# Turning the row maxima on VectorE and laying them under the queries through memory, with the blank rows written behind the first expert's up weights

## The chip, the cores and the metric

The kernel runs on one core of a Trainium2 chip. A core has TensorE (matmuls), VectorE, ScalarE and GpSimd, a sync engine that only issues transfers, and 16 DMA engines that move data between the chip's memory and the core's on-chip memory. Times are device microseconds from start to end of one execution; the median of three runs before the change is 941.17 us (939.94 to 942.25). In what follows PE is TensorE, PEld its weight load, DVE is VectorE, ACT is ScalarE, POOL is GpSimd and SP the sync engine; ACTq and SPq are the instructions with which ACT and SP issue transfers.

## The reference

Eight sequences of 256 tokens, 512 channels, all in float32. One layer: attention of the tokens on a context, then a feed-forward part with a shared expert and eight routed ones, two for each token.

```python
x = x + xattn(layernorm(x), ctx, ctx, Wq, Wk, Wv, Wfc, bfc)   # 32 heads of 16, 8 groups of keys
x = x + ffn(layernorm(x), ...)

# xattn
score = einsum('bhqd,bhkd->bhqk', qh, kh) / sqrt(16)
attn = softmax(score, axis=-1)                                 # subtracts the maximum of each row
out = einsum('bhqk,bhkd->bhqd', attn, vh) ... @ Wfc.T + bfc
# ffn
scores = softmax(h @ gate_weight.T)                            # 8 experts in 4 groups
topk_w, topk_i = group_limited_topk(scores)                    # 2 groups, then 2 experts
routed = sum over the two experts of topk_w * (silu(h @ gate_w.T) * (h @ up_w.T)) @ down_w.T
shared = silu(h @ sh_gate_w.T) * (h @ sh_up_w.T) @ sh_down_w.T
return routed + shared
```

## The kernel before, in words

**Attention.** The work of attention is cut into units: a sequence has eight, made of two groups of key heads, two pairs of query heads and two halves of 128 queries or keys. Each unit k is done twice. In a "max" step (`maxima`, L948) PE computes the scores of 128 queries against 256 keys for eight heads, 16 small matmuls into a PSUM tile `s` of four banks, and DVE takes the negated maximum of each row (L964, the tile `nm`). In an "exp" step (`weights`, L980) PE computes the same scores the other way round, keys on the partitions. The query tile `qT` has a 17th row under the 16 channels of each head, which holds the negated maxima, and the key tile has ones there, so the matmul of 17 rows gives scores from which the maximum has been taken off. ACT takes their exponential (L996). `values` (L1001) multiplies them with the values.

Between the two steps stands `place` (L966): the maxima have the queries on the partitions, but the 17th row needs them along the row. PE turns two blocks of 128 x 8 by a matmul with the identity into a PSUM tile `tn` of the pool `ps_m` (L972), ACT copies 8 x 256 numbers to `nmT` (L976), and ACT issues one transfer into the 17th rows (L978). There are 32 such places, one for every two units.

**The order.** PE, ACT, DVE and SP run in the order in which the program is written; only GpSimd's order is left to the scheduler. The list `order` alternates max and exp steps, the max step four units ahead (LAG = 4), and starts the first two sequences with four max steps in a row. After the matmuls of a step, `beside` (L1330) puts in what is due: for two finished exponentials the products with the values (in max steps after the start), then the places. A place is put in one step after the second maxima of its pair. What else there is to do (projections of later sequences, the output product `close`, the router, the shared expert's `pieces`) stands in a list of stages, and `fill` takes pieces of it, each with a cost in microseconds, until the step is at least `gap - work` and at most `most - work` long. `work` counts what `beside` put in: in an exp step 0.44 for a place. If nothing is ready in the first 44 steps, `warm` puts in two idle matmuls. `others.passed(cost)` tells the stages that time has gone by. The pool `ps_m` has three PSUM buffers, shared by all these pieces and by `tn`.

**The routed experts.** The router sends each token's normed row with `send` (L1173) to two places of a table `rows` in memory, one region for each expert. `plan` works out on DVE where each expert's rows end (`t_end`, L1185) and which blocks of 128 rows there are to do. SP then issues, in this order: the first expert's up weights (L381) and down weights (L384), the first block of rows (`load`, L407 and L413: four transfers of 128 x 128 numbers in 32 x 32 blocks, and a fifth with routing weights and token numbers), blocks and weights of experts 1 and 2, and then, for each expert, 64 blank rows written behind the last one in use (L575, at a row number that SP reads from `t_end`). The loads read the same table as the blank rows are written to, and the row numbers are known on the chip only, so a load waits for blank rows issued before it and blank rows wait for loads issued before them. After that come the shared expert's kept values for the last sequence (L199) and, in `run`, the weights of experts 3, 4 and so on, each set one tile ahead of its block of rows.

`run` goes through the tiles. In each, DVE turns the next block of rows (`turn`, L434), PE computes gate and up (`up`, L468), DVE multiplies them (L485), PE does the down product of the tile before (`down`, L499), and `turn_act` turns the product (L491 on PE, L493 and L494 on DVE). As DVE works in order, the product of tile n (L485) stands behind the turn of block n + 1. At the very end the shared expert's down product for the last sequence is added to what is in memory and written out by SP (L647, L654, L655).

Of the kernel before, what the change touches and what calls it, by code (L numbers as in the profile page):

```python
# [43 lines left out]
F32 = mybir.dt.float32  # L44
I32 = mybir.dt.int32
ENG = mybir.EngineType
# [4 lines left out]
P = 128  # L51
# [33 lines left out]
@with_exitstack  # L85
def xattn_ffn(
    ctx: ExitStack,
    tc: tile.TileContext,
    x: bass.AP,
    ctxT: bass.AP,  # L90
    wq: bass.AP,
    wkv: bass.AP,
    wfc: bass.AP,
    bfc: bass.AP,
    wgate: bass.AP,
    wsg: bass.AP,
    wsd: bass.AP,
    wgu: bass.AP,
    wd: bass.AP,
    out: bass.AP,  # L100
):
    nc = tc.nc

    ctx.enter_context(tc.manual_schedule(engines={ENG.PE, ENG.Activation, ENG.DVE, ENG.SP}))

    keep = ctx.enter_context(tc.tile_pool(name="keep", bufs=1))
    dram = ctx.enter_context(tc.tile_pool(name="dram", bufs=1, space=bass.MemoryType.DRAM))
    ps_m = ctx.enter_context(tc.tile_pool(name="ps_m", bufs=3, space=PSUM))
    right = ctx.enter_context(ExitStack())
    left = ctx.enter_context(ExitStack())  # L110

    ident = keep.tile([P, P], F32, name="ident")
    make_identity(nc, ident)


    t_exp = keep.tile([P, N_PLAN], I32, name="t_exp")
    t_row = keep.tile([P, N_PLAN], I32, name="t_row")
    t_one = keep.tile([P, N_PLAN, N_EXP], F32, name="t_one")
    t_all = keep.tile([P, 1], I32, name="t_all")

    t_end = keep.tile([P, N_EXP], I32, name="t_end")

    blank = dram.tile([R, W], F32, name="blank")
    rows = dram.tile([N_EXP * S_R + P, W], F32, name="rows")


    kept = dram.tile([P, len(SCH), S], F32, name="kept")

    feed = Shared(right, tc, ps_m, wsg, wsd, out, kept)
    tail = attention(  # L130
        left, tc, ps_m, feed, x, ctxT, wq, wkv, wfc, bfc, wgate, out, ident,
        rows, t_exp, t_row, t_one, t_all, t_end, blank,
    )
    left.close()
    routed(
        ctx, tc, ps_m, wgu, wd, wsd, kept, ident,
        rows, t_exp, t_row, t_one, t_all, t_end, blank, out, tail, right,
    )
# [215 lines left out]
def routed(  # L354
# [25 lines left out]
    def up_weights(e):  # L380
        nc.sync.dma_start(wgu_all[:, e], wgu[e])  # L381
# [91 lines left out]
                    stop=(c == NC - 1),  # L473
                )

    def up(i):
        of_expert(i)
        gu = [ps_g.tile([P, F], F32, tag=f"g{k}", name=f"rg{i}_{k}") for k in range(2)]
        for k in range(2):
            product(gu[k], i, slice(k * F, (k + 1) * F))  # L480
        del xTs[i]
        sg = place(work, [P, F], "sg", f"rsg{i}")
        nc.scalar.activation(sg, gu[0], AF.Silu)  # L483
        acts[i] = place(work, [P, F], "act", f"ract{i}")
        nc.vector.tensor_mul(acts[i], gu[1], sg)  # L485
# [76 lines left out]
        add_up(o, i)  # L562

    up_weights(0)
    down_weights(0)

    load(0)
    for e in (1, 2):
        load(e)
        up_weights(e)  # L570
        down_weights(e)

    for e in range(N_EXP):
        to = value(t_end, e, ENG.SP, N_EXP * S_R)
        alone(tc, nc.sync.dma_start(rows[bass.ds(to, R), :], blank).ins)  # L575
    while tail.cost < tail.total - 2 * 0.88:
        tail.step()
    turn(0)
# [30 lines left out]
    def run(tiles):  # L609

        halfs = [n for n, i in enumerate(tiles) if i >= N_EXP + N_FULL]
        when = [N_EXP - 3, *(n + 3 for n in halfs)]
        for n, i in enumerate(tiles):
            if 3 <= n + 2 < len(tiles):
                load(tiles[n + 2])
            if i + 3 < N_EXP:
                up_weights(i + 3)
                down_weights(i + 3)
            for k, at in zip(halfs, when):
                if at == n:  # L620
                    second(tiles[k])
            if n + 1 == len(tiles):
                last(i, tiles[n - 1])
                break
            if n == halfs[-1] + 2:
                down_sh, act_sh = two(len(SCH), D, len(SCH), S)
                nc.sync.dma_start(down_sh, wsd)
                nc.sync.dma_start(act_sh, kept)
            if n > 0:
                turn(tiles[n + 1])  # L630
            up(i)
            if n > 0:
                down(tiles[n - 1])
            else:
                turn(tiles[n + 1])
            turn_act(i)

        sums = []
        for q in range(QC):
            t0 = ((B - 1) * QC + q) * P  # L640
            to = out[t0 : t0 + P, :]
            sums.append((to, work.tile([P, D], F32, tag=f"sum{q}", bufs=1, name=f"sum{q}")))
            nc.sync.dma_start(sums[q][1], to)
        for q, (to, y) in enumerate(sums):
            ps = ps_m.tile([P, D], F32, tag="m", name=f"o{B - 1}_{q}")
            for i in range(len(SCH)):
                nc.tensor.matmul(  # L647
                    ps,
                    lhsT=act_sh[:, i, q * P : (q + 1) * P],
                    rhs=down_sh[:, i],  # L650
                    start=(i == 0),
                    stop=(i == len(SCH) - 1),
                )
            nc.vector.tensor_add(y, ps, y)  # L654
            nc.sync.dma_start(to, y)  # L655
        more()

    full = [N_EXP + k for k in range(N_FULL)]
# [5 lines left out]


def attention(
    ph, tc, ps_m, feed, x, ctxT, wq, wkv, wfc, bfc, wgate, out, ident,
    rows, t_exp, t_row, t_one, t_all, t_end, blank,
):

# [271 lines left out]
    def unit(k):  # L942
# [2 lines left out]
        G, k = divmod(k, UNITS // NG)  # L945
        return b, G, k // QC * 2, k % QC

    def maxima(k):  # L948
        b, G, j0, qc = unit(k)
        qT, kT = qTs[b], kTs[b % DEEP]  # L950
        ps = ps_s.tile([P, 4, 2, S], F32, tag="s", name=f"s1_{b}_{G}_{qc}_{j0}")
        for j in range(2):
            for r in range(4):
                band = slice(32 * r, 32 * r + HD)
                nc.tensor.matmul(  # L955
                    ps[:, r, j],
                    lhsT=qT[band, G, j0 + j, qc * P : (qc + 1) * P],
                    rhs=kT[band, G],
                    start=True,
                    stop=True,  # L960
                )
        if qc == 0:
            nms[b, G, j0] = small.tile([P, QC, 4, 2], F32, tag="nm", bufs=3, name=f"nm{b}_{G}_{j0}")
        nc.vector.tensor_reduce(nms[b, G, j0][:, qc], ps, AX.X, ALU.max, negate=True)  # L964

    def place(k):  # L966

        b, G, j0, _ = unit(k)
        nm = nms.pop((b, G, j0))
        ps = ps_m.tile([P, S], F32, tag="m", name=f"tn{b}_{G}_{j0}")  # L970
        for qc in range(QC):
            nc.tensor.transpose(  # L972
                ps[: 2 * 4, qc * P : (qc + 1) * P], nm[:, qc].rearrange("p r j -> p (r j)"), ident
            )
        row = small.tile([2 * 4, S], F32, tag="nmT", bufs=1, name=f"nmT{b}_{G}_{j0}")
        nc.scalar.copy(row, ps[: 2 * 4])  # L976
        under = qTs[b].rearrange("(r x) g j s -> r x g j s", x=32)[:, HD, G, j0 : j0 + 2]
        nc.scalar.dma_start(under, row)  # L978

    def weights(k):  # L980
        b, G, j0, kc = unit(k)
# [348 lines left out]
    def beside():  # L1330

        for k in to_sum if len(to_sum) == QC else ():
            values(k, ex.pop(k))
            others.passed(1.0)
            b, k = divmod(k, UNITS)
            if k == UNITS - 1:
                closed(b)
            if k % QC == QC - 1:
                to_sum.clear()
        for k in to_place:  # L1340
            place(k)
            others.passed(0.22)
        to_place.clear()

    def closed(b):
# [40 lines left out]
    for i, (what, k) in enumerate(order):  # L1386
        dull = warm if i < 44 else None
        if what == "max":
            if k % UNITS == 0:
                others.finish(projected[k // UNITS])  # L1390

            copy.free = "ACT"
            maxima(k)
            others.passed(1.0)

            gap = 3.2 if len(to_sum) == QC else 2.6
            work = 1.0 * (len(to_sum) == QC) * QC
            beside()
            if k % QC == QC - 1:
                to_place.append(k)  # L1400
            most = 4.6
        else:

            copy.free = "DVE"
            now = k
            ex[k] = weights(k)
            others.passed(1.1)
            gap = 2.1
            work = 1.0 * (len(to_sum) == QC) * QC + 0.44 * len(to_place)
            beside()  # L1410
            to_sum.append(k)
            most = 4.3 if k + LAG < n else 6.0
        others.fill(now, gap - work, most - work, dull)
        if i >= 2:
            next(loads, None)
# [75 lines left out]
```

## Time and profile before

| what | value |
|---|---|
| median of three runs | 941.17 us |
| the profiled execution, in all | 938.76 us |
| its span, first to last instruction | 937.0 us |
| PE busy | 910.8 us (97%) |
| DVE busy | 475.0 us (51%) |
| ACT busy | 182.3 us (19%) |
| POOL busy | 134.3 us (14%) |
| granted TensorE clock over the span | 0.993 |
| attention's units, first max to last exp | about 23 to 567 us |
| routed experts, first to last matmul | 635 to 920 us |

Busy time of PE includes overlap: matmuls are pipelined and their ends are modelled. The page of the profile divides the span in 40 slices of 23.4 us and gives the busy share of each engine in tenths, the clock that TensorE was granted and the busy share of the DMA engines. A view by lines lists groups of equal instructions; a timeline lists single instructions with start and duration, and in square brackets how long the engine had been idle and what released it.

### The profile page before, as it was taken

To read this page: it belongs to the slowest core of one execution; us is meant where nothing else is said; L and a number is where in the kernel's file an instruction comes from. 1 tells how busy PE (TensorE), PEld (TensorE's weight loads), DVE (VectorE), ACT (ScalarE), POOL (GpSimd) and SP (SyncE) were. 2 spreads that over 40 slices of the span, in tenths; PEclk is the share of its full clock that TensorE was granted. 3 is DMA by queue.
4 is the path that set the end of the run, shared out by engine and by line. 5 is a ranking of instruction groups with operands and counts; after the bars stand their busy time and mean duration, and the time that the engine had idled before them with its cause. 6 is when DMAs were issued, how large, how long until landed. Compare 5 with 4: busy or idle time off the path is not lost.

```text
span 937.0 us, 13140 instructions
## 1 busy us (share of the span) xinstructions
PE 910.8 (97%) x4865; PEld 531.1 (57%) x4865; DVE 475.0 (51%) x1063; ACT 182.3 (19%) x222; POOL 134.3 (14%) x171
## 2 busy tenths in 40 slices
PE   9999999999999999999999999999599999999997
PEld 8775565536445554654654544775355555555553
DVE  4554867566755856654675655382233333333331
ACT  1224123223223222222222241101000000000000
POOL 4000100201101101010120121030012212121211
PEclk9999999999999999999999999999799999999999
DMA  6366620201102021011111011069995364644623
GB/s 223 86 180 220 192 46 2 82 6 35 48 13 81 24 46 47 1 53 35 36 48 35 13 48 57 12 219 294 347 341 105 69 164 71 157 78 87 149 38 75
DMA packets 59266, 90.45 MB, mean 97 GB/s; under 512 B 13312, under 2 KB 39680, under 8 KB 57152
## 3 DMA queue, kind: packets, MB, share of 16 engines
q1 hardware_dynamic: 50512, 70.63, 24.7%
q0 software_dynamic: 7648, 17.83, 9.4%
q10 hardware_dynamic: 1040, 1.12, 0.4%
q8 instruction: 41, 0.67, 0.3%
q14 instruction: 25, 0.20, 0.1%
HBM read 57.88 MB, written 27.24 MB: 91 GB/s over the span
## 4 chain that ended last, share of the span: by engine, by line
PE 89%; DVE 4%; DMA 3%; SPq 1%; issue 1%; ACT 1%; POOL 0%; ACTq 0%; DVEq 0%; POOLq 0%
PE rg L468 16%; PE gu L181 14%; PE ro L499 9%; PE o L205 8%; PE s L988 7%; PE s L955 7%; PE fc L1046 6%; PE pq L921 6%; PE av L1007 6%; PE pkv L865 2%; DVE nm L964 1%; PE pkv L854 1%; PE ra L491 1%; PE o L647 1%; PE tn L972 1%; PE warm L1279 1%
## 5 line engine op out<-in xcount | busy, mean ns | idle before, releaser
L964 DVE TENSOR_REDUCE nm<-s 128x8 f32<-128x2048 f32 x64 | 146.6, 2290 | 86.2 <-PE s L955 82.0
L468 PE MATMUL rg<-wgu_all,rxT 128*128 (+2 forms) x552 | 171.3, 464 | 1.1 <-DVE rxT L434 0.9
L181 PE MATMUL gu<-hT,gu_w 128*128 128x256 f32 x704 | 166.6, 385 | 0.0
L996 ACT ACTIVATE ex<-s 128x2048 f32<-128x2048 f32 x64 | 120.1, 1877 | 225.7 <-PE s L988 216.0
L181 PEld LDWEIGHTS gu<-hT,gu_w 128*128 128x128 f32 x704 | 129.1, 190 | 40.9 <-issue 24.6
L468 PEld LDWEIGHTS rg<-wgu_all,rxT 128*128 128x128 f32 (+1 forms) x552 | 100.6, 187 | 56.4 <-issue 8.8
L499 PE MATMUL ro<-wd_all,raT 128*128 (+5 forms) x210 | 96.5, 594 | 0.0
L513 POOL DMA_INDIRECT y<-ry,rid x38 | 58.4, 1537 | 239.5 <-DVE ry L510 156.0
L205 PE MATMUL o<-down,act 128*128 128x512 f32 x168 | 79.6, 604 | 0.3 <-DVE q L346 0.3
L988 PE MATMUL s<-qT,kT 17*128 17x512 f32 x512 | 73.0, 640 | 2.0 <-DVE nm L964 1.9
L955 PE MATMUL s<-kT,qT 16*128 16x256 f32 x1024 | 73.4, 400 | 1.5 <-ACT ex L996 0.8
L483 ACT ACTIVATE rsg<-rg 128x352 f32<-128x352 f32 x34 | 15.8, 464 | 253.2 <-PE rg L468 246.0
L955 PEld LDWEIGHTS s<-kT,qT 16*128 16x128 f32 x1024 | 46.3, 184 | 30.9 <-ACT ex L996 14.1
L499 PEld LDWEIGHTS ro<-wd_all,raT 128*128 128x128 f32 (+3 forms) x210 | 38.4, 186 | 42.9 <-issue 35.5
L921 PE MATMUL pq<-xT,wq_sb 128*128 128x256 f32 x256 | 61.2, 386 | 0.5 <-DVE acc L214 0.3
L1007 PE MATMUL av<-ex,v 128*32 128x512 f32 x512 | 61.5, 598 | 0.0
L1046 PE MATMUL fc<-wfc_sb,o 128*128 128x512 f32 x128 | 60.9, 604 | 0.1
L1173 POOL DMA_INDIRECT rows<-lnf,idx x32 | 31.7, 991 | 201.0 <-DVE idx L1167 190.2
L485 DVE TENSOR_TENSOR ract<-rg,rsg 128x352 f32<-128x352 f32 x34 | 17.8, 523 | 84.0 <-PE rg L468 84.0
L510 DVE TENSOR_SCALAR ry<-ro,rw 128x512 f32<-128x512 f32 x35 | 26.3, 750 | 66.7 <-PE ro L499 66.7
L921 PEld LDWEIGHTS pq<-xT,wq_sb 128*128 128x128 f32 x256 | 46.6, 190 | 14.5 <-issue 6.0
L205 PEld LDWEIGHTS o<-down,act 128*128 128x128 f32 x168 | 29.4, 190 | 35.8 <-issue 34.5
(184 smaller groups left out, 710.0 us busy)
## 6 DMA issues: line engine op xcount, KB each, us to landing
wgu_all<-wgu SPq DMA_DIRECT2D x8, 1408.0 KB
xs<-rows SPq DMA_DIRECT2D x128, 64.0 KB
wd_all<-wd SPq DMA_DIRECT2D x8, 768.0 KB
two<-wgu SPq DMA_DIRECT2D x3, 1408.0 KB
cT<-ctxT SPq DMA_DIRECT2D x8, 512.0 KB
acc<-x SPq DMA_DIRECT2D x16, 256.0 KB
y<-acc SPq DMA_DIRECT2D x16, 256.0 KB
x<-x SPq DMA_DIRECT2D x14, 256.0 KB
```

Of the source, the lines that this page charges most:

```text
L181: nc.tensor.matmul(ps[:, i], lhsT=self.gu[k][:, c, i * P : (i + 1) * P], rhs=hT[:, c], start=(c == 0), stop=(c == NC - 1),)
L205: nc.tensor.matmul(ps, lhsT=act[:, k, q * P : (q + 1) * P], rhs=self.down[:, k], start=(i == 0), stop=(i == len(SCH) - 1),)
L468: nc.tensor.matmul(dst[part], lhsT=xTs[i][:, c, part.start // BAND : part.stop // BAND], rhs=w, start=(c == 0), stop=(c == NC - 1),)
L499: nc.tensor.matmul(o[part], lhsT=aTs[i][:fn, fc, part], rhs=w, start=(fc == 0), stop=(fc == len(FCH) - 1),)
L513: nc.gpsimd.indirect_dma_start(out=out, out_offset=bass.IndirectOffsetOnAxis(ap=to, axis=0), in_=y[part], in_offset=None, compute_op=ALU.add,)
L921: nc.tensor.matmul(ps[:, i], lhsT=wq_sb[:, c, part], rhs=xT[:, c], start=(c == 0), stop=(c == NC - 1),)
L955: nc.tensor.matmul(ps[:, r, j], lhsT=qT[band, G, j0 + j, qc * P : (qc + 1) * P], rhs=kT[band, G], start=True, stop=True,)
L964: nc.vector.tensor_reduce(nms[b, G, j0][:, qc], ps, AX.X, ALU.max, negate=True)
L988: nc.tensor.matmul(ps[:, r], lhsT=kT[band, G, kc * P : (kc + 1) * P], rhs=qT[band, G, j0 : j0 + 2], start=True, stop=True,)
L996: nc.scalar.activation(ex, ps, AF.Exp, scale=HD**-0.5)
L1007: nc.tensor.matmul(av[32 * r : 32 * r + 32], lhsT=vs[b % DEEP][:, kc, 4 * G + r], rhs=ex[:, r], start=(kc == 0), stop=(kc == QC - 1),)
L1046: nc.tensor.matmul(ps, lhsT=o[:, c, qc * P : (qc + 1) * P], rhs=wfc_sb[:, c], start=(c == 0), stop=(c == NC - 1),)
```

## The change

It has four parts.

1. `place` no longer uses PE, PSUM and an ACT copy. The maxima of a pair of units are written to one of three fixed tiles of 128 x 32, set to zero once by GpSimd, in 16 of its 32 columns. DVE turns the tile in blocks of 32 x 32, and ACT issues a transfer of the whole turned tile (128 pieces of 32 numbers) to a buffer in memory. One step later a new function `take` lets ACT issue a second transfer, from that buffer into the 17th rows. The filler's account of a place (0.44 in `work`, 0.22 in `passed`) is gone.
2. The eight writes of blank rows stand between the first expert's up weights and its down weights.
3. The first tile's turn of the product (`turn_act` of tile 0) stands between the gate and the up product of tile 1.
4. The last writes of the output are issued by ACT.

```diff
-    def up(i):
+    def up(i, between=None):
         of_expert(i)
...
         for k in range(2):
             product(gu[k], i, slice(k * F, (k + 1) * F))
+            if k == 0 and between is not None:
+                turn_act(between)
...
     up_weights(0)
+
+    for e in range(N_EXP):
+        to = value(t_end, e, ENG.SP, N_EXP * S_R)
+        alone(tc, nc.sync.dma_start(rows[bass.ds(to, R), :], blank).ins)
     down_weights(0)
 
     load(0)
...
         load(e)
         up_weights(e)
         down_weights(e)
-
-    for e in range(N_EXP):
-        to = value(t_end, e, ENG.SP, N_EXP * S_R)
-        alone(tc, nc.sync.dma_start(rows[bass.ds(to, R), :], blank).ins)
     while tail.cost < tail.total - 2 * 0.88:
...
-            if n > 0:
-                turn(tiles[n + 1])
-            up(i)
+            turn(tiles[n + 1])
+            up(i, tiles[0] if n == 1 else None)
             if n > 0:
                 down(tiles[n - 1])
-            else:
-                turn(tiles[n + 1])
-            turn_act(i)
+                turn_act(i)
...
             nc.vector.tensor_add(y, ps, y)
-            nc.sync.dma_start(to, y)
+            nc.scalar.dma_start(to, y)
...
+    nm_tiles = [late.tile([P, BAND], F32, name=f"nm{i}") for i in range(3)]
+    for t in nm_tiles:
+        nc.gpsimd.memset(t, 0.0)
+
     def maxima(k):
...
         if qc == 0:
-            nms[b, G, j0] = small.tile([P, QC, 4, 2], F32, tag="nm", bufs=3, name=f"nm{b}_{G}_{j0}")
-        nc.vector.tensor_reduce(nms[b, G, j0][:, qc], ps, AX.X, ALU.max, negate=True)
+            nms[b, G, j0] = nm_tiles[k // QC % len(nm_tiles)]
+        nm = nms[b, G, j0][:, : 4 * 2 * QC].rearrange("p (r j c) -> p r j c", j=2, c=QC)
+        nc.vector.tensor_reduce(nm[:, :, :, qc], ps, AX.X, ALU.max, negate=True)
 
     def place(k):
 
         b, G, j0, _ = unit(k)
         nm = nms.pop((b, G, j0))
-        ps = ps_m.tile([P, S], F32, tag="m", name=f"tn{b}_{G}_{j0}")
-        for qc in range(QC):
-            nc.tensor.transpose(
-                ps[: 2 * 4, qc * P : (qc + 1) * P], nm[:, qc].rearrange("p r j -> p (r j)"), ident
-            )
-        row = small.tile([2 * 4, S], F32, tag="nmT", bufs=1, name=f"nmT{b}_{G}_{j0}")
-        nc.scalar.copy(row, ps[: 2 * 4])
-        under = qTs[b].rearrange("(r x) g j s -> r x g j s", x=32)[:, HD, G, j0 : j0 + 2]
-        nc.scalar.dma_start(under, row)
+        turned = small.tile([P, BAND], F32, tag="nmT", name=f"nmT{b}_{G}_{j0}")
+        nc.vector.transpose(turned, nm)
+        where = dram.tile([BAND, P // BAND, BAND], F32, name=f"nm{b}_{G}_{j0}_rows")
+        nc.scalar.dma_start(where.rearrange("x a i -> a x i"), turned)
+        to_take.append((b, G, j0, where))
+
+    def take(b, G, j0, where):
+
+        under = qTs[b].rearrange("(r x) g j s -> r x g j s", x=BAND)[:, HD, G, j0 : j0 + 2]
+        where = where[: 4 * 2 * QC].rearrange("(r j c) a i -> r j (c a i)", j=2, c=QC)
+        nc.scalar.dma_start(under, where)
+
+    to_take = []
...
             if k % QC == QC - 1:
                 to_sum.clear()
+        for some in to_take:
+            take(*some)
+        to_take.clear()
         for k in to_place:
             place(k)
-            others.passed(0.22)
         to_place.clear()
...
-            work = 1.0 * (len(to_sum) == QC) * QC + 0.44 * len(to_place)
+            work = 1.0 * (len(to_sum) == QC) * QC
```

## The prediction, made before the change was built

> **What bounds the kernel.** I read the page's slices first, then the chain that ended last, then the stretches in which its releaser is not PE.
>
> ```profile
> PE   9999999999999999999999999999599999999997
> PEclk9999999999999999999999999999799999999999
> DMA  6366620201102021011111011069995364644623
> PE 89%; DVE 4%; DMA 3%; SPq 1%; issue 1%; ACT 1%; POOL 0%; ACTq 0%; DVEq 0%; POOLq 0%
> ```
>
> PE is busy nearly always and makes 89% of the chain, so PE time removed is won unless a slot waits for something else anyway. There is one hole: slice 29, where the clock falls too, in the middle of a stretch with all DMA engines busy. So the kernel has two places to look at: PE's own work in attention, and the passage to the experts.
>
> In attention the timeline shows one place (L972 to L978) between an exp step and the next max step:
>
> ```profile
> 299.20 1.14 PE L988 MATMUL s<-qT,kT 17*128 17x512 f32 x8 [0.78 <-DVE nm L964]
> 300.27 0.38 PE L972 MATMUL tn<-ident,nm 128*8 128x128 f32 x2
> 300.41 1.88 ACT L996 ACTIVATE ex<-s 128x2048 f32<-128x2048 f32 x1 [1.57 <-PE s L988]
> 300.49 0.51 PE L1103 MATMUL lg<-chunks,parts 128*128 128x8 f32 x4
> 302.18 0.34 ACT L976 COPY nmT<-tn 8x256 f32<-8x256 f32 x1
> 302.56 0.55 ACTq L978 DMA_DIRECT2D qT<-nmT  x1
> 302.82 1.15 PE L955 MATMUL s<-kT,qT 16*128 16x256 f32 x16
> 303.89 1.92 PE L1007 MATMUL av<-ex,v 128*32 128x512 f32 x16
> 307.78 0.38 ACT L193 ACTIVATE sg<-gu 128x256 f32<-128x256 f32 x1 [4.42 <-PE gu L181]
> ```
>
> The two turns start at 300.27 and the next matmul at 300.49: 0.22 us of PE, though their rows give 0.38. ACT reaches the place only after the exponential, and then has little to do until 307.78.
>
> At the passage, PE, DVE and SP:
>
> ```profile
> 653.86 2.74 PE L499 MATMUL ro<-wd_all,raT 128*128 128x512 f32 x6
> 667.68 0.90 PE L491 MATMUL ra<-ident,ract 128*128 128x128 f32 x3 [11.08 <-DVE ract L485]
> 666.38 0.71 DVE L434 STREAM_TRANSPOSE rxT<-xs 128x512 f32<-128x512 f32 x1 [16.11 <-DMA xs<-rows]
> 628.73 1.79 SPq L407 DMA_DIRECT2D xs<-rows  x4
> 634.25 0.43 SPq L381 DMA_DIRECT2D wgu_all<-wgu  x1
> 644.42 8.06 SPq L575 DMA_DIRECT2D rows<-blank  x8
> 652.57 0.53 SPq L199 DMA_DIRECT2D kept<-act  x1
> 655.80 2.15 SPq L407 DMA_DIRECT2D xs<-rows  x4
> 650.00:652.00 2.00, 2.00 (x8) 1.33 (x7) 0.27 (x2) 0.31 (x1) 1.61 (x1) 1.00 0.42 134
> ```
>
> PE stands 11.08 us for tile 2's product (L485), which DVE holds behind the turn of block 3 (L434), which waits for that block's load. The load was issued at 655.80, after the eight blank writes, and queued behind the kept values and the weights of expert 3. While SP issued the blanks the weight stream ran dry: 134 GB/s and a DMA share of 0.42 at 650 to 652, against some 340 GB/s and 1.0 from 668 to 700.
>
> **Part 1, the maxima.** It removes 32 times two turns on PE: 32 x 0.22 = 7.0 us (the chain's pieces of 0.31 us would give 9.9). With them go 32 ACT copies of 0.35 us, off the path, and one use of `ps_m` each.
>
> Added on DVE: 32 turns of 128 x 32. The trace has no such size; L1020 turns 128 x 512 in 0.708 and L1031 128 x 256 in 0.445 us, so 1.03 ns a column and 445 - 224 x 1.03 = 215 ns. That is 6.9 us on an engine that is 51% busy: nothing on the path in the 28 places after an exp step, where DVE has ended its maximum (PE waited for it at 299.20). It can't be a gain. Four places, in the runs of four max steps, differ: DVE's turn stands there behind the next maximum of 2.29 us, ACT's transfer waits for it, and the projections' copies (L346) stand behind that. Between 0 and 1.6 us each, since PE has three buffers to go on with; I take 0.2, in sum 0.8.
>
> Added on ACT's queue: one more transfer for each place, 32 x 0.545 us of issue (L978), on an engine that is 19% busy, and a wait: `take` can't be issued before the first transfer has landed in memory. Behind it on ACT stand the copies and the shared expert's activations (L193) of that max step, then the next exponential. Nearest rows: the scatter of 128 rows to the same memory landed after 2.8 to 3.2 us, the last blank write after 3.81 us (651.97 to 655.78). With 3.0 us: the exponential ends at 302.29, the issue at 302.84, it lands at 305.8, `take` is out at 306.4; the first ACT work behind is ready at 307.78, because the max step with a `take` is also the one with PE's 1.92 us of values. So 0, with 1.4 us of cover. The Trainium skill speaks against this ("DMA: Bandwidth & Descriptors", Specifications and Anatomy of one DMA): pieces under 512 B make the engine read, modify and write, and most of a transfer's fixed 2 us is the receipt of the write, heaviest in HBM, where its latency section allows 2 us of access at high load. The new transfer is 128 pieces of 128 B, written to just that memory. By the page's high load, as an estimate, 2 + 2 = 4 us, which the cover still holds; 6 us would not. I take the row's 3.0 and keep the rest for a rival. The second transfer has the cover of about five steps of 4.2 us (543 us for 128 steps) before its exp step, so its landing costs nothing; in the first run of maxima about two steps, still more than 3 us.
>
> The filler: exp steps with a place now ask for 0.44 more work. PE's total work stays, but where nothing is ready an idle matmul pair comes in place of the turns, 0.33 us of PE each. The trace has warm-ups in one of the eight such steps among the first 44; I take two, 0.7 us. GpSimd's three small memsets lie in a pause of 0.48 us before its first variance (8.14 to 8.62 us): nothing.
>
> Part 1: -7.0 + 0.8 + 0.7 = -5.5 us; ends -9.9 and -3, ACT's wait aside.
>
> **Part 2, the blank rows.** They go past the down weights of expert 0, the first three blocks and the weights of 1 and 2 on SP. `t_end` is ready at 619.90. Seven steps of the old loop took 644.42 to 651.97, 1.08 us each, so the last issue ends at about 628.4, when the down weights could go anyway (628.28). But the first load now waits for eight landed blanks: 627.9 + 3.0 to 3.8 = 631.3 instead of 628.73. SP then issues ten transfers of 0.45 us before expert 1's weights: 635.8 instead of 634.25 (there the stretch took 5.5 us, with waits for landed loads that are now behind it). So the stream starts 1.5 us later, and PE's first tile about 2 us later.
>
> In exchange 1.08 MB of writes and the dry spell are gone from the stream. By 644 it had moved 3.1 of the 4.6 MB of blocks and weights 1 and 2; the rest at 0.36 MB/us ends at 648.1, now at 649.6. From the issue of the kept values to the turn of block 3 it took 652.57 to 666.38, 13.8 us, of which about 0.8 was start on an idle queue. So block 3 is turned at 649.6 + 13.0 = 662.6, against 666.38: 3.8 us earlier. Can PE use it? Its own work would have it there at about 659, late start included. After that the weights of 3 to 7 keep DMA full until 704; block 8 was turned at 706.42, 40.0 us after block 3, and PE was waiting for it (0.12 us idle at 708.54). The same bytes follow at the same rate, so tile 8 starts 3.8 us earlier, and from there PE is continuous. The clock: it fell to 0.50 from 662 to 672, and tile 3's products took 6.48 instead of 4.74 us. The skill ("TensorE: Matmul & The Clock Gate", Part 1) has half rate after one idle window of about 3.4 us; the remaining stall, 658 to 664, is longer, so the 1.7 us are not won by the page, while by the row, where the fall came some 4 us into the hole, they might be. Either way the stream sets tile 8: 0 in the sum. Ends: 0 (SP's delay of 2.6 us kept whole, the dry spell half refilled) and -14.5 (the stalls of 11.08, 0.94 and 0.69 us and the 1.74 of slow clock all gone).
>
> **Parts 3 and 4.** Tile 0's turn behind the gate product removes a wait of 0.69 us (640.76), but it lies ahead of the stall at 658, which swallows it: 0, or -0.7 if that stall is gone. ACT issues the last write in 0.55 us where SP took 0.34: +0.2.
>
> **Sum:** -5.5 - 3.8 + 0.2 = -9.1 us. The span of 937.0 becomes 927.9 and the profiled 938.76 becomes 929.7. The median of the runs is 2.4 above the profiled one: 941.2 - 9.1 = 932.1, I say 932.
>
> **Rivals.**
>
> *One part gives nothing.* The filler pays back PE's 7 us with idle work or waits on maxima and exponentials (PE stood idle for 4.7 us between 20 and 560), or the late first load eats the dry spell. For: warm-ups exist, and SP's queue is in order. Against: from 200 us on PE always has pieces. 941.2 - 3.6 = 937.6, or 941.2 - 5.3 = 935.9.
>
> *The stall goes whole.* If blocks 1 to 3 land as PE needs them, 7.0 + 14.5 = 21.5: 920. Against it: 15 MB of weights at 340 GB/s can't be moved earlier than SP starts.
>
> *ACT is held by the `take`, slower.* Place: each max step with a `take`. From 1.4 us over the 3.0 on, activations are late; `ps_m` lets PE run about 1.3 us further. At 6 us of landing, 0.3 us for each of 32 steps cancels the 9 us; at 6.5 us, 0.8 x 32 = 26, which gives 941.2 - 9.1 + 26 = 958; at 6.2 us about 947. For: DMA is 58% busy from 20 to 100 us, and ACT's queue has twice the transfers, and SP's waits have one for a transfer of ACT's (L886 for `qT<-nmT`, 1.1 us) that it has no data from, so transfers may wait for older ones too. Against: after 100 us DMA is at 0.1 to 0.2.
>
> **Chances.** As summed: 0.58, with 927 to 936. One part nothing: 0.15. Stall whole: 0.09. ACT held: 0.18. The range takes in all but most of the last and the far end of the third: 922 to 941. Three thousandths, 2.8 us, is what a measurement here can tell. Faster: 0.58 + 0.09 + 0.11 = 0.78; within: 0.05; slower: 0.17.
>
> **What would show it.** PE's rows have no `tn`, and its busy time falls by some 12 us of row time. DVE has 32 turns of about 0.2 us. In the waits, L193 and L346 on ACT have no new releaser among the transfers; if they have, the ACT rival holds. SP issues blanks from 620 less 5.5 us on, block 3 is turned some 26 us after the first routed product starts (662.6 - 637; 31.3 before), PE's hole is 5 to 7 us, and the DMA share stays near 1.0 from the first routed weights to expert 7. I am wrong if attention's last exponential isn't 4 us or more earlier, or if the hole is still over 10 us.

## The result: 7 us slower, and the profile after

The changed kernel takes 948.05 us (median of five runs, 947.84 to 950.7), against 941.17: a ratio of 1.0083, with a 95% interval of 1.0065 to 1.0102. The profiled execution is one of the longer ones, 950.29 us with a span of 948.6. I had said 932.

The page of the changed kernel, slices and chain:

```profile
PE   9999999999999999999999999898799999999997
PEclk9999999999999899999999999999899999999999
DMA  6356540122010011011111011048996454544623
PE 79%; DMA 9%; DVE 6%; ACT 2%; SPq 2%; issue 1%; POOL 0%; ACTq 0%; POOLq 0%; DVEq 0%
```

The deep hole of slice 29 has become shallower, a 7 there and an 8 in slice 28. Slice 26, at the end of attention, has an 8 that is new: a wait of 2.43 us for DVE at 595.97. And the clock now has a dent at slice 14, in the middle of attention. PE's part of the chain fell from 89% to 79%: more of the time is set by what PE waits for. First the passage to the experts, from the timelines of PE, DVE and SP:

```profile
651.57 9.06 PE L468 MATMUL rg<-wgu_all,rxT 128*128 128x352 f32 x24 [2.90 <-DVE rxT L434]
678.34 0.90 PE L493 MATMUL ra<-ident,ract 128*128 128x128 f32 x3 [4.79 <-DVE ract L487]
677.04 0.71 DVE L434 STREAM_TRANSPOSE rxT<-xs 128x512 f32<-128x512 f32 x1 [9.82 <-DMA xs<-rows]
635.17 9.28 SPq L570 DMA_DIRECT2D rows<-blank  x8
644.77 0.35 SPq L384 DMA_DIRECT2D wd_all<-wd  x1
646.46 1.76 SPq L407 DMA_DIRECT2D xs<-rows  x4
651.12 0.43 SPq L381 DMA_DIRECT2D wgu_all<-wgu  x1
659.77 0.33 SPq L199 DMA_DIRECT2D kept<-act  x1
661.09 3.36 SPq L407 DMA_DIRECT2D xs<-rows  x4
```

The first tile waits 2.90 us instead of 0.94 for its late load, and tile 2's product 4.79 instead of 11.08. Tile 0 begins 16.5 us later than before (651.57 against 635.07); tile 8's products begin at 720.35 against 708.66, 11.7 us later. So from tile 0 to tile 8 the passage gained 4.8 us. Against that stands the late first load, 2.0 us ahead of tile 0, which leaves the passage a gain of 2.8. Attention lost the rest: PE's last product ahead of tile 0 ends at 648.67, against 634.13 before, 14.5 us later.

In attention, three places in the changed kernel's timeline. The first is an ordinary one:

```profile
218.09 1.88 ACT L1005 ACTIVATE ex<-s 128x2048 f32<-128x2048 f32 x1 [0.63 <-PE s L997]
218.17 0.52 ACTq L978 DMA_DIRECT2D nm_rows<-nmT  x1
220.11 0.52 ACTq L985 DMA_DIRECT2D qT<-nm_rows  x1
220.15 1.15 PE L959 MATMUL s<-kT,qT 16*128 16x256 f32 x16
```

The transfer to memory is issued 0.08 us after the exponential has begun, not after its end, and the second follows 1.94 us after the first: out of the way before the max step begins. The second place is in the run of four max steps at the start:

```profile
40.59 2.29 DVE L969 TENSOR_REDUCE nm<-s 128x8 f32<-128x2048 f32 x1 [1.71 <-PE s L959]
42.80 0.20 DVE L976 STREAM_TRANSPOSE nmT<-nm 128x32 f32<-128x32 f32 x1
43.03 0.54 ACTq L978 DMA_DIRECT2D nm_rows<-nmT  x1
43.61 1.07 ACT L346 COPY xT<-tx 128x512 f32<-128x512 f32 x2 [3.56 <-DVE nmT L976]
44.74 1.53 PE L920 MATMUL pq<-xT,wq_sb 128*128 128x256 f32 x4 [2.06 <-ACT xT L346]
46.20 2.09 PE L997 MATMUL s<-qT,kT 17*128 17x512 f32 x8
```

The turn stands behind the next maximum, ACT's transfer behind the turn, the copy of `xT` behind the transfer, and PE waits 2.06 us for the copy. The eight matmuls at 46.20 then take 2.09 us where they took 1.14. The third is in the middle:

```profile
312.38 2.49 POOL L1048 TENSOR_TENSOR acc<-acc,bfc_sb 128x512 f32<-128x512 f32 x2 [30.13 <-DVE sg L194]
313.92 1.00 DVE L1089 TENSOR_TENSOR gtg<-best 128x32 f32<-128x32 f32 x1
315.51 0.19 DVE L1095 TENSOR_REDUCE rankg<-gtg 128x8 f32<-128x32 f32 x1
315.73 2.29 DVE L969 TENSOR_REDUCE nm<-s 128x8 f32<-128x2048 f32 x1
318.07 1.83 PE L997 MATMUL s<-qT,kT 17*128 17x512 f32 x8 [1.90 <-DVE nm L969]
```

This one has nothing to do with the place: a maximum stands behind nine operations of the router on DVE (312.67 to 315.70), because the router's pieces now fall into that step. PE waits 1.90 us. What follows both stalls is in the view of stretches, whose third number from the end is the granted clock:

```profile
48.00:52.00 4.00, 4.00 (x13) 3.07 (x10) 0.00 (x0) 1.88 (x1) 0.00 (x0) 0.50 0.40 99
318.00:322.00 4.00, 3.93 (x13) 2.13 (x14) 2.77 (x13) 1.88 (x1) 0.00 (x0) 0.55 0.01 4
```

PE is as good as always busy there, at half its clock.

I added up, from both profiles, what lies ahead of tile 0. PE's idle stretches over 0.1 us between 20 us and the end of attention's tail: 13.7 us after, 4.3 before (+9.4). Clock not granted there, from stretches of 1 us: 45 to 53, 229 to 233 and 318 to 326, 8.5 us in sum, none before (+8.5). Idle matmuls: 80 against 68, six pairs of 0.33 us (+2.0). The late first load: +2.0. The turns gone: 32 times 0.12, as found below (-3.8). The sum is 18.1; 16.5 were measured.

### The profile page after: what moved, and what is told of

Same layout as the page of the kernel before. It is cut to its first block, busy times and chain, and to the rows that moved or that the text cites. A ratio compares the mean times of both kernels' runs of the same rounds, so it can differ in the third digit from the quotient of the medians.

```text
span 948.6 us, 13116 instructions
## 1 busy us (share of the span) xinstructions
PE 918.2 (97%) x4813; PEld 535.3 (56%) x4813; DVE 480.5 (51%) x1090; ACT 175.7 (19%) x195; POOL 133.7 (14%) x174
## 4 chain that ended last, share of the span: by engine, by line
PE 79%; DMA 9%; DVE 6%; ACT 2%; SPq 2%; issue 1%; POOL 0%; ACTq 0%; POOLq 0%; DVEq 0%
PE gu L181 15%; PE rg L468 13%; PE o L205 8%; PE ro L501 7%; PE s L997 7%; PE s L959 6%; PE pq L920 5%; PE fc L1055 5%; PE av L1016 5%; DMA xs<-rows 3%; DVE nm L969 2%; DMA wd_all<-wd 2%; PE pkv L853 1%; PE pkv L864 1%; ACT ex L1005 1%
## 5 line engine op out<-in xcount | busy, mean ns | idle before, releaser
L468 PE MATMUL rg<-wgu_all,rxT 128*128 (+2 forms) x552 | 173.4, 468 | 3.1 <-DVE rxT L434 2.9
L181 PE MATMUL gu<-hT,gu_w 128*128 128x256 f32 x704 | 171.6, 393 | 0.0
L181 PEld LDWEIGHTS gu<-hT,gu_w 128*128 128x128 f32 x704 | 131.4, 193 | 51.3 <-issue 32.2
L920 PE MATMUL pq<-xT,wq_sb 128*128 128x256 f32 x256 | 63.8, 398 | 2.4 <-ACT xT L346 2.4
```

Source lines behind the costliest of these rows:

```text
L181: nc.tensor.matmul(ps[:, i], lhsT=self.gu[k][:, c, i * P : (i + 1) * P], rhs=hT[:, c], start=(c == 0), stop=(c == NC - 1),)
L468: nc.tensor.matmul(dst[part], lhsT=xTs[i][:, c, part.start // BAND : part.stop // BAND], rhs=w, start=(c == 0), stop=(c == NC - 1),)
L920: nc.tensor.matmul(ps[:, i], lhsT=wq_sb[:, c, part], rhs=xT[:, c], start=(c == 0), stop=(c == NC - 1),)
```

## The experiments

**Theories.** A, the order: the edit of the filler's account (`work` without its 0.44, no 0.22 passed) puts other pieces beside the maxima, and the stalls, the slow clock after them and more idle matmuls follow. B, the place: DVE's turn, ACT's two transfers and the wait between them hold other work back, whatever the order. In both, moving the blank rows gains. Each ratio below is against the kernel before, run in the same session (medians of 941.4 to 941.9 us).

**Blank rows alone**, the kernel before with that one move:

```diff
     up_weights(0)
+    for e in range(N_EXP):
+        to = value(t_end, e, ENG.SP, N_EXP * S_R)
+        alone(tc, nc.sync.dma_start(rows[bass.ds(to, R), :], blank).ins)
     down_weights(0)
```

> The kernel before with only the eight writes of blank rows moved behind the first expert's up weights. Tile 8 of the routed experts began 11.7 us later in the changed kernel, tile 0 16.5 us later, so the passage itself gained 4.8. Every theory that puts the loss into attention expects 941.2 - 4.8 = about 936.5 us, with a hole on PE ahead of tile 2's product of 5 to 7 us (11.08 before). If the passage's gain came from something else (the clock, tile 0's turn of the product), 940 to 942.

Measured: 936.36 us, ratio 0.9940 (0.9921 to 0.9959). Its profile has PE's stall at 664.18, of 4.03 us, and tile 8 begins at 705.25, 3.4 us earlier than before. The move alone gains 5.0 us by the medians of its session (941.40 before), 5.6 by the ratio.

**Blank rows back**, the changed kernel without that move:

> The changed kernel with the blank rows back behind the weights of experts 1 and 2. If moving them gained 4.8 us, 948.1 + 4.8 = about 953 us and a hole of some 11 us on PE; if the passage gained by the other parts, 948.

Measured: 954.52 us, ratio 1.0144 (1.0110 to 1.0179), and the hole is back, 12.19 us at 678.65. The four runs spread from 949.83, the profiled one, to 957.23. So the move gains about as much inside the changed kernel (6.5 us by the medians), and the rest of the change costs 13 us.

**The account kept** in the changed kernel:

```diff
             place(k)
+            others.passed(0.22)
...
-            work = 1.0 * (len(to_sum) == QC) * QC
+            work = 1.0 * (len(to_sum) == QC) * QC + 0.44 * len(to_place)
```

> The changed kernel with the filler's account of a place as before (0.44 in the work, 0.22 passed). PE's order in attention is then that of the kernel before, without the two turns. Theory A, the order: the account made the loss, since other pieces come to stand beside the maxima; then the turns' 7.0 us and the passage's 4.8 are won and only the stall in the first run of maxima stays (2.06 us and 3.4 of half clock): 941.2 - 11.8 + 5.5 = about 935 us. Theory B, the place itself: DVE's turn, ACT's two transfers and the wait between them hold copies back whatever the order; then 945 to 949.

Measured: 935.11 us, ratio 0.9949 (0.9922 to 0.9976).

**The account alone taken out** of the kernel before, turns on PE and all:

```diff
             place(k)
-            others.passed(0.22)
...
-            work = 1.0 * (len(to_sum) == QC) * QC + 0.44 * len(to_place)
+            work = 1.0 * (len(to_sum) == QC) * QC
```

> The kernel before, its turns on PE kept, with only the filler's account of a place taken out (0.44 and 0.22). PE's order in attention is then that of the changed kernel, with the two turns. Theory A, the order: attention lost 11.7 us in the changed kernel; with 7.0 won by the turns and 5.5 lost in the first run of maxima the order costs 13.2, so 941.2 + 13.2 = about 954 us. Theory B, the place itself: 941 to 943.

Measured: 959.28 us, ratio 1.0200 (1.0166 to 1.0233), 5 us above what A expected. In attention these two kernels have, matmul for matmul, the PE order of the kernel before and of the changed kernel, without and with the turns. The two settle it for A: the order costs 13 us with the new place (948.05 against 935.11) and 18 with the old one, while the new place with the old order (935.11, with parts 3 and 4) stands where the blank rows alone do (936.36). Of the 18.8 us by which the old place with the new order comes later to tile 0 than before (653.89 against 635.07), by the same sums as above, 9.7 are PE's idle time, 6.8 clock and 2.0 idle matmuls. Its stalls of over 1 us wait for the same operations as the changed kernel's, all but the one at 44.7, which it doesn't have; one at 465.39 is longer here (1.29 us against 0.40). The one behind the router, from its timeline:

```profile
312.34 2.49 POOL L1039 TENSOR_TENSOR acc<-acc,bfc_sb 128x512 f32<-128x512 f32 x2 [31.14 <-DVE total L1119]
315.58 2.29 DVE L964 TENSOR_REDUCE nm<-s 128x8 f32<-128x2048 f32 x1
317.92 1.59 PE L988 MATMUL s<-qT,kT 17*128 17x512 f32 x8 [2.54 <-DVE nm L964]
```

So a kernel that still turns on PE has it too, at 2.54 us.

This kernel and the one with the blank rows back have the same order and the same blank rows. They differ in the place and in parts 3 and 4, and the new place is the faster one: 954.52 against 959.28, 4.8 us, with intervals that overlap a little. So in sum the place itself costs nothing; in the old order it gains 1.3 us (935.11 against 936.36), which is within the intervals.

**What a pair of turns is worth.** With the same order, steps can be laid side by side, from the start of a step's scores to the start of the next step's:

| exp step with a place | old place, old order | new place, old order | old place, new order | new place, new order |
|---|---|---|---|---|
| the 32nd step | 3.14 | 3.19 | 3.98 | 3.86 |
| the 44th | 3.14 | 3.20 | 3.55 | 3.38 |
| the 88th | 4.31 | 4.20 | 4.31 | 4.19 |
| the 104th | 5.69 | 5.57 | 4.31 | 4.20 |

Where PE sets the step, the turns' removal gains 0.11 to 0.12 us (0.17 in the 44th step of the new order). Where the step is at its shortest, it loses 0.05 to 0.06. Over all 28 exp steps with a place the new place takes 2.1 us less in the old order and 4.3 us less in the new one. The timeline of PE in such a step, before and then with the account kept:

```profile
170.46 1.14 PE L988 MATMUL s<-qT,kT 17*128 17x512 f32 x8
171.54 0.38 PE L972 MATMUL tn<-ident,nm 128*8 128x128 f32 x2
171.75 1.88 PE L205 MATMUL o<-down,act 128*128 128x512 f32 x4
173.68 1.15 PE L955 MATMUL s<-kT,qT 16*128 16x256 f32 x16
```

```profile
174.71 1.14 PE L997 MATMUL s<-qT,kT 17*128 17x512 f32 x8
175.78 1.98 PE L205 MATMUL o<-down,act 128*128 128x512 f32 x4
177.98 1.15 PE L959 MATMUL s<-kT,qT 16*128 16x256 f32 x16 [0.22 <-ACT ex L1005]
```

The next scores need the PSUM tile that ACT's exponential is reading, and that takes 3.2 us from the start of the step. The two turns were part of what PE did meanwhile; without them it waits 0.22 us. Taking the 0.44 out of the account made the filler ask for 2.1 us in such a step instead of 1.66, which is three pieces of 0.88 and not two. Before, 16 exp steps are no longer than 3.3 us; in the changed kernel one is.

**The turn early.** The account kept, and DVE's turn written directly behind the second maximum:

```diff
         nc.vector.tensor_reduce(nm[:, :, :, qc], ps, AX.X, ALU.max, negate=True)
+        if qc == QC - 1:
+            turned = small.tile([P, BAND], F32, tag="nmT", name=f"nmT{b}_{G}_{j0}")
+            nc.vector.transpose(turned, nms.pop((b, G, j0)))
+            turns[b, G, j0] = turned
...
-        nm = nms.pop((b, G, j0))
-        turned = small.tile([P, BAND], F32, tag="nmT", name=f"nmT{b}_{G}_{j0}")
-        nc.vector.transpose(turned, nm)
+        turned = turns.pop((b, G, j0))
...
+    turns = {}
```

> The changed kernel with the account kept, and DVE's turn written directly behind the second maximum of a pair and not one step later; the two transfers stay where they are. If the stall of 2.05 us in the fifth step comes from ACT's transfer, which waits for a turn that stands behind the next maximum, it goes, and so does the half clock after it (3.4 us lost in the profile of the account kept): 935.1 - 2 to - 5.4 = 930 to 933 us. Rival: ACT is then held as long by the second transfer, which waits for the first to land; then 935.

Measured: 932.74 us, ratio 0.9913 (0.9897 to 0.9929), the fastest version of all. From its timeline, the same spot as in the changed kernel above:

```profile
38.15 0.21 DVE L972 STREAM_TRANSPOSE nmT<-nm 128x32 f32<-128x32 f32 x1
38.70 0.55 ACTq L980 DMA_DIRECT2D nm_rows<-nmT  x1
39.82 2.29 DVE L969 TENSOR_REDUCE nm<-s 128x8 f32<-128x2048 f32 x1 [1.46 <-PE s L959]
40.30 1.07 ACT L346 COPY xT<-tx 128x512 f32<-128x512 f32 x2 [1.02 <-PE tx L825]
```

The transfer is out before the next maximum begins, the copy waits for its own matmuls only, and the stall is gone. By the medians that is 2.4 us; the two intervals just touch, so its size is not sharp.

**The turn early with the account gone:**

> The changed kernel as it is (account gone), with DVE's turn directly behind the second maximum. The stall of 2.06 us at 44.7 goes and perhaps the half clock behind it; the stalls that the filler's order makes stay: 948.1 - 2 to - 5.5 = 943 to 946 us. If the place, and not the order, were what costs, it would come near the 930 to 933 of the same kernel with the account kept.

Measured: 948.74 us, ratio 1.0080 (1.0063 to 1.0097): no gain at all, so I expected too much. The profile is of the fastest of its four runs, 945.32 us. The stall at 44.7 is gone from the profile, but the one at 81.41 of the changed kernel (1.27 us) has become 4.14 us at 79.11. There a copy of `q` stands on DVE behind the moments of a sequence, and these behind its load. The load lands at 78.86 in the changed kernel and at 76.51 here; DVE waits 2.36 us for it there and 5.19 here, since the work ahead of it is done earlier:

```profile
76.51 0.69 DVE L807 BATCH_NORM_STATS2 sta<-x 128x6 f32<-128x512 f32 x1 [5.19 <-DMA x<-x]
78.37 0.69 DVE L346 COPY q<-pq 128x512 f32<-128x512 f32 x1
79.11 3.78 PE L853 MATMUL pkv<-cT,wkv_sb 128*128 128x256 f32 x8 [4.14 <-DVE q L346]
```

So in this order the time that the early turn saves is spent waiting for that load.

**The 0.44 alone.** The changed kernel with the 0.44 put back and the 0.22 not:

> The changed kernel with only the 0.44 in the work of an exp step put back, not the 0.22 passed. PE's order is then that of the kernel with the whole account, but for one exchange of pieces. If the 0.44 is what set the order, 935 us as with the whole account; if the 0.22 matters too, between 935 and 948.

Measured: 937.15 us, ratio 0.9939 (0.9916 to 0.9961), the same as with the whole account within the intervals. The 0.44 is what set the order.

**A smaller account.** As the turn early, with 0.30 for 0.44:

> As the kernel with the account kept and the turn early, but with 0.30 in place of 0.44 for a place. An exp step asks for 2.1 less the account, a piece counts 0.88: up to 0.34 that takes three pieces, above it two. With 0.30 PE's order is, but for a few exchanges, that of the changed kernel; with 0.38 it is already that of the account kept. If the third piece is what costs, about 946 to 949 us; if the size of the account counts by degrees, about 938, two thirds of the way back to 933.

Measured: 951.41 us, ratio 1.0073 (1.0049 to 1.0097), a little above the 946 to 949 of a third piece. Two thirds of the account give back nothing: what counts is not its size but whether it changes the order, and at 0.30 an exp step with a place still asks for a third piece.

**Two pieces in all exp steps.** The turn early, no account, and

```diff
             ex[k] = weights(k)
             others.passed(1.1)
-            gap = 2.1
+            gap = 1.7
```

> As the changed kernel with the turn early and no account, but every exp step asks for 1.7 of filler and not 2.1: two pieces in all of them, with a place or without. It has 28 idle matmuls where the kernels with the old order have 68, 6.6 us of PE less; but more exp steps end at the 3.2 us that the exponential sets, some 0.2 us of waiting each. If a third piece costs because work is used up early, 927 to 933 us; if only the chance of what stands ahead of a maximum on DVE decides, anywhere from 930 to 950.

Measured: 935.63 us, ratio 0.9935 (0.9913 to 0.9956). That is 13 us better than the same kernel with three pieces (948.74) and no better than the old order. It lies above the 927 to 933 of the first expectation and inside the 930 to 950 of the second, so it doesn't settle whether a third piece costs as such or by the chance of what it puts where: the first expectation counted on 28 idle matmuls, and the trace has 56, 4.6 us more of PE at 0.33 a pair. Six of the nine runs took 933.5 to 935.9 us and three 940.4 to 941.1. The profile is of one of these three, and it has a stall of 3.23 us that shows my rival in the flesh:

```profile
84.43 0.52 ACTq L987 DMA_DIRECT2D qT<-nm_rows  x1
85.05 1.88 ACT L1008 ACTIVATE ex<-s 128x2048 f32<-128x2048 f32 x1 [5.66 <-DMA nm_rows<-nmT]
86.98 1.14 PE L1000 MATMUL s<-qT,kT 17*128 17x512 f32 x8 [3.23 <-ACT ex L1008]
```

In the stretch where the shared weights are loaded, the small transfer to memory was issued at 73.06, and the second one, which waits for its landing, went out at 84.43. ACT, held by the second, was idle for 5.66 us. The scores were done at 81.79, so the exponential began 3.3 us late.

**Parts 3 and 4 back as before**, in the kernel with the account kept and the turn early:

```diff
-            turn(tiles[n + 1])
-            up(i, tiles[0] if n == 1 else None)
+            if n > 0:
+                turn(tiles[n + 1])
+            up(i)
             if n > 0:
                 down(tiles[n - 1])
-                turn_act(i)
+            else:
+                turn(tiles[n + 1])
+            turn_act(i)
...
-            nc.scalar.dma_start(to, y)
+            nc.sync.dma_start(to, y)
```

> As the kernel with the account kept and the turn early, with tile 0's turn of the product and the last writes as before. If the 0.69 us wait ahead of tile 0's turn is swallowed by the later stall, no difference within 1 us; if the shorter stall no longer swallows it, 0.7 to 1.5 us slower than that kernel.

Measured: 933.33 us, ratio 0.9903 (0.9886 to 0.9920), against 0.9913 with them: no difference beyond the intervals.

## Why the prediction was wrong

**The step that failed is "The filler".** I put the account's edit down as two more idle pairs, 0.7 us, with PE's total work unchanged. It costs 13 us with the new place and 18 with the old. My own sign says the same: attention's last exponential was to be 4 us or more earlier, and it begins 12.8 us later (579.90 against 567.09). I had read that the steps with a place "ask for 0.44 more work" and left it at that. With pieces of 0.88 it is one piece more in nearly every such step, so the same work is done in another order from the first sequence on. What comes of it isn't seen in any sum over PE's work: maxima and copies that stand behind router or moment operations on DVE, and PE's clock halved after some of these stalls (9.4 us of idle time, 8.5 of clock and 2.0 of idle matmuls in the changed kernel's profile). Five kernels with three pieces in such a step take 948 to 959 us; five with the new place and two pieces take 933 to 937. Apart from a few exchanges, though, these are only three different orders, so it is shown that this order costs, and not that any third piece would. Which stall belongs to which moved piece I read from timelines only.

**The turns were mis-sized.** I took 0.22 us from the starts of neighbouring matmuls. Removed, they gain 0.11 to 0.12 where PE sets the step, since the matmul after them took 0.1 us longer in their absence, and lose 0.05 where the exponential sets it. The 7.0 us were 4.3 in the order of the changed kernel and 2.1 in the old one, by the sums over 28 steps. My sentence "unless a slot waits for something else anyway" was the right doubt; I didn't count how many slots were at that point: in the old order, 14 of the 28.

**The four places in the runs of maxima** I put at 0.8 us in all, 0 to 1.6 each. One of them cost 2.06 us of idle PE, and in the profiles of the changed kernel and of the account kept another 3.4 of clock. The mechanism was right, the size was not, and the clock I had weighed only at the passage.

**The blank rows were right.** Tile 8 was to start 3.8 us earlier, late load included. Alone, the move brings it 3.4 us earlier in the profile and gains 5.0 us by the medians; in the changed kernel it is 2.8, counted from the end of PE's work ahead of tile 0. The late first load was forecast at about 2 us and came at 2.0, the remaining hole at 5 to 7 and came at 4.0 to 4.8, and block 3's turn some 26 us after the first routed product, which came at 25.5. One reading was off: before, the clock fell 5.1 us into the hole (which begins at 656.60; the stretch 661 to 662 was granted 0.86), not some 4. Nothing in the sum rests on it, and the slow stretch was not won: tile 3's products, after the hole, took 7.18 us instead of 6.68.

**Parts 3 and 4** were forecast at 0 and +0.2 and show nothing beyond the intervals.

**The rivals.** Of the rivals, "one part gives nothing" ended at 938, since I priced the filler's idle work and waits at no more than the 7 us to be won; that they can exceed it was the point missed. The rival that was slower was not this one: ACT's second transfer does hold ACT now and then, and in one kernel PE for 3.23 us, but in the changed kernel none of PE's stalls of over 1 us comes from it. In the ordinary place shown above the second transfer went out 1.94 us after the first, so the landing took less than the 3.0 assumed. The Trainium skill ("DMA: Bandwidth & Descriptors", Anatomy of one DMA) gives its fixed 2 us for transfers that GpSimd issues; ACT's transfer there agrees with it. Its 2 us of HBM access at high load, and my 4 us made of it, do not account for the one landing that took about 11.4 us (73.06 to 84.43). The DMA engines were full then (a share of 1.09 from 76 to 80), and no run separates small pieces and a loaded memory from a plain wait behind the big loads.

**What would be worth keeping:** the blank rows' move, the account of 0.44, and the turn directly behind the maximum, which gives 932.74 us. Of its gain of some 8 us about 5 are the blank rows'.

## What to carry to other kernels

A number in a planner's account is not a cost that can be deleted with the instruction it stood for: compare it with the size of the pieces, and look whether it crosses a step, since one piece more in each slot is another program. Before counting an instruction's time as won, look at what ends its slot: if that is another engine's work on the same buffer, the instruction was cover. And when an instruction is written one step later in an engine's order, see what now stands ahead of it there.

## What the runs showed that I had not expected

**The clock falls after stalls shorter than the page says.** Stalls of 2.06, 1.47 and 1.90 us in the changed kernel were followed by 6.8, 3.4 and 6.8 us at half clock, 8.5 us lost. I had cited an idle window of about 3.4 us from the Trainium skill ("TensorE: Matmul & The Clock Gate", Part 1). The page also says that this window runs free and that the ramp varies from run to run. The kernel with the blank rows back, which has the same order in attention, agrees: its profile has stalls of 2.06, 1.47 and 2.10 us at the same pieces and full clock through them, and 3.4 us of half clock after one of 2.50 us at 588.57. It is the profile of the fastest of its four runs, which were granted 0.981 to 0.989 over the span. So a short stall may cost nothing more or several microseconds, and executions of one kernel differ by that.

The twelve profiles show more. In each of them the clock changes only at points that are 3.41 us apart or a whole number of times that, so that the span falls into windows of 3.41 us, as long as the page's, and these lie differently against the work in every profile. The stall of 2.06 us lies in one window in the changed kernel, and is cut in two in the kernel with the blank rows back (the windows with the stall and the next one, first of the changed kernel, then of the other):

```profile
41.92:45.33 3.41, 1.30 (x7) 1.06 (x8) 1.08 (x2) 1.07 (x2) 0.00 (x0) 1.00 0.84 207
45.33:48.75 3.42, 3.42 (x12) 1.24 (x11) 0.00 (x0) 0.40 (x1) 0.00 (x0) 0.50 0.48 178
40.25:43.67 3.42, 1.86 (x15) 1.48 (x13) 2.23 (x2) 0.57 (x2) 0.00 (x0) 1.00 0.73 115
43.67:47.08 3.41, 2.86 (x15) 1.67 (x16) 0.00 (x0) 1.09 (x3) 0.00 (x0) 1.00 0.79 305
```

PE is idle for 2.11 us of the first window, and the clock falls at its end; in the third it is idle for 1.56 us, and the clock stays. Over all twelve profiles, the first four windows of each left out, all 39 windows at full clock with more than 1.95 us idle are followed by half clock; of the 38 with 0.9 to 1.7 us idle one is; of the nine in between, five. So what counts in these traces is PE's idle time within one window, and some 1.7 to 1.95 us of it are enough. No run was made to test this.

**A transfer's issue doesn't wait for the activation ahead of it.** In the changed kernel ACT issued the transfer at 218.17, 0.08 us after an activation of 1.88 us had begun. The copy that stood there before began 1.77 us after the activation's start (302.18 against 300.41), near its end.

**A DVE operation of 0.18 us took 1.00** (L1089, above) while GpSimd was adding 128 x 512 numbers, and 0.97 in the kernel with the account alone taken out, beside the same add. It ended at 314.92, when GpSimd's adds did (314.87). Over the traces of all twelve kernels this operation falls beside that add 19 times and takes 0.73 to 1.27 us in 18 of them, and 0.2 us wherever it doesn't. Here it is 0.8 us longer than usual, ahead of a maximum for which PE waited 1.90 us. The new order puts the router beside GpSimd's add more often, three times in the changed kernel and once before.
